# Three lanes of a four-layer graph network, emitted in finer turns

## The chip, the cores and the metric

The kernel runs on one core of a Trainium2 chip. The time is that of the device in microseconds (us), and the figure for a kernel is the median over several runs. A profile shows one execution. In it PE is the matrix engine (PEld: its weight loads, which overlap its matmuls), DVE the vector engine, ACT the scalar engine, POOL the GpSimd engine, and SP the engine that issues most DMAs. Each engine works through its own queue of instructions; semaphores order the engines among each other.

## The reference

There are 16 graphs of N = 1024 nodes with D = 128 features, each with a sparse weighted adjacency matrix `adj` (about 1.6% of the entries, and the diagonal, are not zero). Four layers follow each other. Each normalizes x over its features, takes the positive part as h, and adds to x what its network makes of h:

```python
# layer 0: mean over neighbours of h, joined to h, times W, relu
sum_neighbors = einsum('bid,bij->bjd', h, adj) / adj.sum(-1)
x += relu(concat([h, sum_neighbors]) @ W.T + b)
# layer 1: row-normalized adj times h, times W, leaky relu
x += leaky(einsum('bnm,bmf->bnf', adj / adj.sum(-1), h) @ W.T + b)
# layer 2, twice: a score for every pair of nodes, weighted messages, an update
hid = relu(a[:, :, None] + b[:, None, :] + be1)      # N x N x D
upd = adj * sigmoid(hid @ We2 + be2)
msg = upd @ x;  x = layernorm(x + relu([x, msg] @ Wu1 + bu1) @ Wu2 + bu2)
# layer 3: attention over neighbours
att = softmax(where(A > 0, leaky((Wh1 + Wh2.T) * A), -inf));  x += elu(att @ Wh)
```

## The kernel before

**Tiles.** The nodes of a graph are T = 8 tiles of P = 128. The pairs (t, u) of tiles are 36 buckets: 28 off the diagonal, 8 on it. In a bucket a row has few entries, so layer 2 is not computed for all pairs of nodes. `build` makes, for each bucket, four one-hot matrices in fp8: `on` and `om` say which node of tile t, and which of tile u, each entry (edge) has; `onT` and `omT` are their transposes. An off-diagonal bucket holds up to 320 such columns, a diagonal one 480.

**The work of layer 2** goes by nine groups of four buckets and twice over them, since layer 2 has two rounds. For each bucket, `gather` multiplies the node terms (`part`, split in two fp16 halves) by the one-hot matrices into a PSUM bank `pre` (of which there are two), four matmuls a bank; ACT takes the positive part to `hid`, and DVE the remainder to its second half. Off the diagonal this is done in both directions, d = 0 and 1. `dots` sums four `hid` tiles over the features into `sc`. `ends` applies tanh into `srow`. One group later `scores` transposes it (`pt`), and DVE multiplies `onT` and `omT` by the scores, tile by tile, into `val`: eight such multiplications an off-diagonal group, four a diagonal one. `scatter`, one quarter at a time, turns `val` back into a matrix of tiles in the bank `p`, DVE multiplies it by the loaded `adj` into `upd`, and `messages`, called later from the list `late`, adds up the messages in the banks `acc0` and `acc1`. `behind` is what calls these for the group before. `between` is the update of one half of the nodes between the two rounds: it loads the old features `xm`, evacuates the messages with `off`, runs `update` (two matmul stages `h` and `xn`, transposes `tx`, a normalization) and transposes the result (`tp`, L1146).

**Three lanes.** Three graphs are worked on at a time, each by a generator:

- `main` (lane m): layer 2 of graph b.
- `first` (lane a): layers 0 and 1 of graph b+1, and then `build` for it. For each of eight row tiles it loads `at` (rows) and `ct` (columns), transposes `at` on PE (`tn`), writes the transpose to DRAM, marks the buckets in `has`, and multiplies neighbours (`nb`), whose result DVE adds to `own`. Lane a has a single PSUM bank in the steady state, so `tn`, `nb`, and later `pr`, `pn`, `pq` and `pm` of `build` use it in turn.
- `last` (lane c): the second update of graph b-1, then layer 3, in which a strip `a` of adjT is loaded, DVE and ACT make `e` of it, and PE multiplies it (`hp`).

**What sets the order.** `weave` runs the three generators together. A generator's `yield us` says how much of its own time the turn just emitted is worth; divided by the lane's total (`MAIN_US`, `FIRST_US`, `LAST_US`) it gives the lane's progress, and the lane that is least far goes next. The sums of the turns are close to these constants, so all three lanes reach their end nearly together:

```python
least = min(out_of, key=lambda v: v[:2])
us = next(least[2], None)
...
least[0] += us / least[3]
```

This is not yet the order on the engines. The framework's planner gives each engine its queue, taking instructions as they become ready by its own costs, and among the ready ones those that were emitted first. It also hands out the buffers: two for `pre`, one for lane a, two rows of 512 KB for lane a's loads.

**Head and tail.** For graph 0 lane a runs alone up to the start of `build`; after graph 15's layer 2, lane c runs alone.

The lines that the prediction speaks of: L743 `tn`, L288 `nb`, L313 `own`, L260 transposes of the normalized input, L817 `pn` and `pm`, L850 `pq`, L854 `omT`, L986 `pre`, L1003 `hid` on DVE, L1018 `sc`, L1075 `val`, L1097 `p`, L1105 `upd`, L1114 `msg`, L342 `h`, L716 loads of `xm`, L1146 `tp`.

Of the kernel before, what the change touches and what calls it, by code (L numbers as in the profile page):

```python
# [42 lines left out]
MAIN_US = 243.0  # L43
FIRST_US = 118.0
LAST_US = 75.0
# [6 lines left out]
def tile_four_gnn_layers(  # L52
# [136 lines left out]
    class Layers:  # L189
# [74 lines left out]
        def pre_ln(self, xt, name, dst=None, dstT=None):  # L264

            h = self.scratch(f"h_{name}") if dst is None else dst
            self.normal(xt, h, AF.Relu, name)
            return self.transposed(h, name, dstT)
# [33 lines left out]
        def layer0_own(self, xt, name):  # L302
            hT = self.pre_ln(xt, f"0_{name}")
            z = self.scratch(f"z0_{name}")
            own = self.scratch(f"own_{name}")
            for sl, ps in self.both(hT, wT[:, 0:2], f"0_{name}"):
                nc.scalar.activation(z[:, sl], ps[:, :, 1], AF.Copy)
                nc.vector.tensor_add(own[:, sl], ps[:, :, 0], over_t(b0_bc, 2))
            return z, own
# [10 lines left out]
        def layer1(self, xt, strip, rdeg, name):  # L320
            hT = self.pre_ln(xt, f"1_{name}")
            yield 6
            z = self.scratch(f"z1_{name}")
            for sl, ps in self.by_node(hT, wT[:, 2], f"z1_{name}"):
                nc.scalar.activation(z[:, sl], ps, AF.Copy)
            o = self.scratch(f"o1_{name}")
# [57 lines left out]
        def layer3(self, xt, row, name):  # L384

            hT = self.pre_ln(xt, f"3_{name}")
            yield 6
            wh = self.scratch(f"wh_{name}")
            for sl, ps in self.by_node(hT, w3_sb, f"wh_{name}"):
                nc.scalar.activation(wh[:, sl], ps, AF.Copy)  # L390
            wh1, wh2 = self.score_terms(hT, 0, name)
# [70 lines left out]
    class Lane(Layers):  # L462
# [5 lines left out]
        def layer3(self, xt, strip, zero, name):  # L468
# [3 lines left out]
            hT = self.pre_ln(xt, f"3_{name}")  # L472
            yield 6
            wh = self.wide(f"wh_{name}")
            nc.vector.memset(wh[:, :, D : D + 1], 1.0)
            for sl, ps in self.by_node(hT, w3_sb, f"wh_{name}"):
                nc.scalar.activation(wh[:, sl, :D], ps, AF.Copy)
            wh2, wh1 = self.score_terms(hT, 1, name)
            yield 6
# [3 lines left out]
            for lo, hi in L3_ROWS:  # L483
# [4 lines left out]
                for k in range(0, T, 2):  # L488
# [13 lines left out]
                    nc.vector.scalar_tensor_tensor(e, at, 0.0, e, op0=OP.is_gt, op1=OP.mult)  # L502
                    for i in range(2):
# [5 lines left out]
                    yield 1.2 * n  # L509
# [18 lines left out]
    class Edges:  # L528
# [190 lines left out]
        def first(self, b):  # L719
# [4 lines left out]
            z, own = lane.layer0_own(xt, name)  # L724
            yield 8
# [6 lines left out]
            for t in range(T):  # L732
# [8 lines left out]
                for ks, ps in lane.halves(f"tn_{b}_{t}"):  # L741
                    for i, k in enumerate(ks):
                        nc.tensor.transpose(ps[:, i], at[:, k], ident)  # L743
                    nc.scalar.activation(turned[:, ks[0] : ks[-1] + 1], ps, AF.Copy)
                nc.sync.dma_start(self.columns(s.adjT, t), turned)
# [8 lines left out]
                yield 2  # L754
# [9 lines left out]
            s.xT = self.kept(lane.pre_ln(xt, f"2_{name}", dst=s.xf), "xT", f"xT0_{b}")  # L764
            s.x = self.kept(xt, "x", f"xk_{b}")
            yield 6
# [56 lines left out]
        def build(self, s, has, name):  # L823
# [4 lines left out]
            yield 0  # L828
            for g, grp in enumerate(GROUPS):
# [11 lines left out]
                nc.scalar.activation(rank, pr, AF.Copy)  # L841
                for i, (t, u) in enumerate(grp):
                    nm = f"{name}_{t}_{u}"
                    on = self.rows_hot(s, t, u, nm)
                    pn = self.turned(on, ck, f"pn_{nm}")
                    onT = self.hot_tile("onT", t, u, ck * P, nm)
                    nc.scalar.activation(onT, pn[:, : ck * P], AF.Copy, saturate=False)  # L847
                    pq = self.a.one(f"pq_{nm}").rearrange("p (k m) -> p k m", m=P)
# [9 lines left out]
                    )  # L858
                    pm = self.turned(omT, ck, f"pm_{nm}")
# [6 lines left out]
                    yield 1.3  # L866
# [14 lines left out]
        def round(self, s, l, name, before, after):  # L881
# [7 lines left out]
            def behind(i):  # L889
                if i == 0 and old:  # L890
                    old.scores()
                    parts.extend((old, part) for part in range(Q))
                elif parts:
                    g, part = parts.pop(0)
                    g.scatter(part)
                if len(self.late) > 1:
                    self.late.pop(0)()

# [4 lines left out]
            for k in range(len(GROUPS)):  # L903
# [9 lines left out]
                for i in range(Q):  # L913
                    g.gather(i)
# [3 lines left out]
                    behind(i)  # L918
                    g.dots()
                    yield 2.8  # L920
                    if (k, i) == (FIRST + 2, 1):
                        flush()
                        beside = after()
                    yield from islice(beside, 2)
                g.ends()
                old = g
            for i in range(Q + 2):
                behind(i)
# [483 lines left out]
```

## Time and profile before

| | |
|---|---|
| median of 3 runs | 5530.16 us (5516.44 to 5542.56) |
| the profiled execution, its own time | 5528.34 us |
| its span, first to last instruction | 5526.6 us |
| mean granted clock of PE | 0.987 |
| DMA, mean over the span | 100 GB/s |
| starts of `main` for graphs 5, 6 and 7 (its first load) | 1801.0, 2138.8, 2476.5 us |

The last row shows the period: 337 us a graph from graph 2 on, with three graphs in work at any moment. In what follows the head is 0 to 140 us, the tail 5400 us to the end, and the body what lies between. Rows of the view by stretches give the start and end of a stretch, its length, then for PE, PEld, DVE, ACT and POOL the busy time and the number of instructions, and at the end the granted clock, the share of DMA engines busy, and GB/s. Rows of the view of waits name who waited, for whom, the idle time in us, how often, and the longest. In the view in order of time the number in brackets is the idle time of the engine ahead of that row, and what ended it. An f32 matmul is two instructions in the trace.

### The profile page before, as it was taken

To read this page: it belongs to the slowest core of one execution; us is meant where nothing else is said; L and a number is where in the kernel's file an instruction comes from. 1 tells how busy PE (TensorE), PEld (TensorE's weight loads), DVE (VectorE), ACT (ScalarE), POOL (GpSimd) and SP (SyncE) were. 2 spreads that over 40 slices of the span, in tenths; PEclk is the share of its full clock that TensorE was granted. 3 is DMA by queue.
4 is the path that set the end of the run, shared out by engine and by line. 5 is a ranking of instruction groups with operands and counts; after the bars stand their busy time and mean duration, and the time that the engine had idled before them with its cause. 6 is when DMAs were issued, how large, how long until landed. Compare 5 with 4: busy or idle time off the path is not lost.

```text
span 5526.6 us, 113576 instructions
## 1 busy us (share of the span) xinstructions
PE 5037.3 (91%) x45109; PEld 3719.3 (67%) x45109; DVE 4304.6 (78%) x10759; ACT 3054.6 (55%) x6790; POOL 184.9 (3%) x137
## 2 busy tenths in 40 slices
PE   5999999999999999999999999999999999999996
PEld 4676766667676666666766666676766767666664
DVE  4777787878879787787877878778787887978886
ACT  4555564655647555465555646556465564655543
POOL 0000000000000000000000000000000000000000
PEclk8999999999999999999999999999999999999998
DMA  6242424243242433424334142432424324243111
GB/s 174 62 136 87 121 68 137 76 125 101 84 140 66 125 96 92 131 66 120 98 102 124 56 139 81 122 106 71 140 72 128 97 85 133 67 124 95 54 63 51
DMA packets 740139, 554.56 MB, mean 100 GB/s; under 512 B 32272, under 2 KB 686352, under 8 KB 739600
## 3 DMA queue, kind: packets, MB, share of 16 engines
q1 hardware_dynamic: 734496, 545.58, 33.6%
q8 instruction: 356, 5.83, 0.4%
q10 hardware_dynamic: 5104, 1.65, 0.1%
q14 instruction: 183, 1.50, 0.1%
HBM read 446.44 MB, written 100.66 MB: 99 GB/s over the span
## 4 chain that ended last, share of the span: by engine, by line
PE 47%; DVE 27%; DMA 9%; ACT 9%; issue 4%; POOL 3%; SPq 0%; ACTq 0%; DVEq 0%; POOLq 0%
PE pre L986 11%; DVE val L1075 10%; PE p L1097 6%; DMA at<-in_adj_dram 4%; DVE hid L1003 4%; PE nb L288 4%; PE msg L1114 4%; PE bb L296 3%; PE sc L1018 3%; DMA a<-adjT 2%; DVE omT L854 2%; PE hp L505 2%; POOL st L243 2%; PE h L342 2%; PE tn L743 2%
## 5 line engine op out<-in xcount | busy, mean ns | idle before, releaser
L1003 DVE SCALAR_TENSOR_TENSOR hid<-pre,hid 128x320 f16<-128x320 f32 (+1 forms) x2048 | 993.0, 504 | 294.9 <-ACT hid L1002 283.9
L1002 ACT ACTIVATE hid<-pre 128x320 f16<-128x320 f32 (+1 forms) x2048 | 900.7, 454 | 501.3 <-PE pre L986 473.4
L986 PEld LDWEIGHTS <-part 128*128 128x128 f16 x8192 | 753.4, 98 | 450.5 <-issue 236.2
L986 PE MATMUL pre<-on,part 128*128 128x320 fp8e4 (+1 forms) x4096 | 966.2, 309 | 71.6 <-DVE hid L1003 60.6
L986 PE MATMUL pre<-om,part 128*128 128x320 fp8e4 (+1 forms) x4096 | 994.3, 309 | 0.0
L1114 PE MATMUL msg<-upd,xf 128*128 128x128 f32 (+3 forms) x3008 | 613.6, 323 | 2.2 <-DVE upd L1105 2.2
L1075 DVE TENSOR_TENSOR val<-onT,u 128x384 f32<-128x384 fp8e4 (+1 forms) x1152 | 607.8, 580 | 4.0
L1097 PE MATMUL p<-val,omT 128*128 128x128 f16 x6528 | 534.2, 219 | 29.8 <-DVE val L1075 27.7
L1097 PEld LDWEIGHTS <-omT 128*128 128x128 fp8e4 x6528 | 436.7, 96 | 84.4 <-DVE val L1075 34.4
L1075 DVE TENSOR_TENSOR val<-omT,u 128x384 f32<-128x384 fp8e4 x896 | 439.2, 549 | 0.0
L861 ACT ACTIVATE om<-pm 128x320 fp8e4<-128x320 f32 (+1 forms) x576 | 268.9, 467 | 294.4 <-PE pm L817 285.8
L1114 PEld LDWEIGHTS msg<-upd,xf 128*128 128x128 f32 x3008 | 414.2, 191 | 25.6 <-DVE upd L1105 13.9
L1105 DVE SCALAR_TENSOR_TENSOR upd<-p,adj 128x512 f32<-128x512 f32 x512 | 348.5, 681 | 82.4 <-PE p L1097 82.2
L1097 PE MATMUL p<-val,onT 128*128 128x128 f16 x4480 | 374.1, 219 | 1.4 <-DVE upd L1105 1.4
L847 ACT ACTIVATE onT<-pn 128x384 fp8e4<-128x384 f32 (+1 forms) x576 | 297.6, 517 | 102.7 <-PE pn L817 82.8
L1039 ACT ACTIVATE srow<-sc,be_s,down 128x128 f32<-128x128 f32 (+2 forms) x512 | 259.7, 540 | 168.2 <-PE sc L1018 166.9
L505 PE MATMUL hp<-wh,e 128*128 128x129 f32 x2048 | 318.3, 285 | 22.3 <-DVE e L502 22.3
L1097 PEld LDWEIGHTS <-onT 128*128 128x128 fp8e4 x4480 | 304.6, 97 | 36.9 <-issue 8.8
L505 PEld LDWEIGHTS hp<-wh,e 128*128 128x128 f32 x2048 | 275.5, 195 | 51.9 <-DVE e L502 29.6
L804 ACT ACTIVATE far<-iota_off,mid 128x384 f16<-128x384 f16 x448 | 269.5, 625 | 39.9 <-DVE on L808 34.3
L288 PE MATMUL nb<-z,ct 128*128 128x128 f32 x2048 | 279.3, 282 | 12.4 <-DMA ct<-in_adj_dram 11.9
L1018 PE MATMUL sc<-hid,slide 128*32 128x320 f16 (+1 forms) x4096 | 268.3, 315 | 18.2 <-DVE hid L1003 15.7
(220 smaller groups left out, 8106.8 us busy)
## 6 DMA issues: line engine op xcount, KB each, us to landing
at<-in_adj_dram SPq DMA_DIRECT2D x128, 512.0 KB, 4.3
ct<-in_adj_dram SPq DMA_DIRECT2D x128, 512.0 KB, 4.6
adjT<-tn SPq DMA_DIRECT2D x128, 512.0 KB, 5.1
l<-adjT SPq DMA_DIRECT2D x128, 512.0 KB, 4.2
adj<-adjT SPq DMA_DIRECT2D x256, 256.0 KB, 3.4
a<-adjT SPq DMA_DIRECT2D x128, 384.0 KB, 3.5
adj<-adjT SPq DMA_DIRECT2D x448, 64.0 KB, 2.1
adj<-adjT SPq DMA_DIRECT2D x192, 128.0 KB, 2.6
```

The lines of the kernel that those rows point to most:

```text
L288: nc.tensor.matmul(ps, mat[:, k], z[:, k], start=(k == 0), stop=(k == T - 1))
L505: nc.tensor.matmul(sums[:, t], e[:, i, t * P : (t + 1) * P], wh[:, k + i, : D + 1], start=False, stop=True, skip_group_check=True,)
L804: nc.scalar.activation(far[:, : ck * P], self.iota[t == u][:, : ck * P], AF.Abs, bias=s.mid[:, i : i + 1])
L847: nc.scalar.activation(onT, pn[:, : ck * P], AF.Copy, saturate=False)
L986: nc.tensor.matmul(pre[:, :c], path.parts[node // Q][:, k, node % Q, v], hot[:, :c], start=(hot is on and k == 0), stop=(hot is om and k = ...
L1002: nc.scalar.activation(hid[:, 0, :c], pre[:, :c], AF.Relu)
L1003: nc.vector.scalar_tensor_tensor(hid[:, 1, :c], pre[:, :c], 0.0, hid[:, 0, :c], op0=OP.max, op1=OP.subtract)
L1018: ins = nc.tensor.matmul(self.sc[g * G : (g + 1) * G, : self.c], self.path.slide[:, self.l, G - 1 - r : 2 * G - 1 - r], self.hid[self.done ...
L1075: nc.vector.tensor_tensor(pair[:, i % 2, :ck], right[:, :ck], v.to_broadcast([P, ck, P]), op=OP.mult)
L1097: nc.tensor.matmul(self.ps[d][:, i], left[:, k], halves[:, k, :, h], start=(k, h) == terms[0], stop=(k, h) == terms[-1],)
L1105: nc.vector.scalar_tensor_tensor(upd, self.ps[d], S_SCALE, self.adj[:, d * Q : (d + 1) * Q], op0=OP.add, op1=OP.mult,)
L1114: nc.tensor.matmul(self.msg[h][:, (lo - h * Q) * P : (hi - h * Q) * P], self.xf[mb // Q][:, mb % Q], up, start=False, stop=True, skip_grou ...
```

## The change

The computation stays the same. Turns are cut smaller and given new worth, and some instructions change their place:

- `pre_ln` becomes a generator: the normalization is one turn, the transposes another. `layer0_own`, `layer1` and `layer3` hand its turns on.
- In `first`, `tn` yields after each half, and `nb` follows the second half in the same turn.
- In `build`, a bucket is five turns rather than one.
- In lane c's layer 3, a turn ends between the making of `e` and its matmuls, and between the two halves of these.
- In `round`, a gather of two directions, the scatter, the late messages and the dots are turns of 0.2 to 0.6, where before they were one turn of 2.8. `between` for half 0 is begun two gathers earlier (at group FIRST + 1, last bucket), but only up to a new `yield 0` behind its load.
- `last` issues the loads of both halves, and `off` for both, ahead of the first update; before, `main` did `off` at its end, and each half's load stood ahead of its own update.
- The three constants are set to the new sums.

```diff
-MAIN_US = 243.0
-FIRST_US = 118.0
-LAST_US = 75.0
+MAIN_US = 184.0
+FIRST_US = 115.0
+LAST_US = 70.0
...
-        def pre_ln(self, xt, name, dst=None, dstT=None):
+        def pre_ln(self, xt, name, dst=None):
             h = self.scratch(f"h_{name}") if dst is None else dst
             self.normal(xt, h, AF.Relu, name)
-            return self.transposed(h, name, dstT)
+            yield 2
+            self.hT = self.transposed(h, name)
+            yield 2
...
         def layer1(self, xt, strip, rdeg, name):
-            hT = self.pre_ln(xt, f"1_{name}")
-            yield 6
+            yield from self.pre_ln(xt, f"1_{name}")
             z = self.scratch(f"z1_{name}")
-            for sl, ps in self.by_node(hT, wT[:, 2], f"z1_{name}"):
+            for sl, ps in self.by_node(self.hT, wT[:, 2], f"z1_{name}"):
                 nc.scalar.activation(z[:, sl], ps, AF.Copy)
+                yield 1
...
                     nc.vector.scalar_tensor_tensor(e, at, 0.0, e, op0=OP.is_gt, op1=OP.mult)
+                    yield 0.4 * n
                     for i in range(2):
                         for t in range(n):
                             nc.tensor.matmul(
...
-                    yield 1.2 * n
+                        yield 0.4 * n
...
-            z, own = lane.layer0_own(xt, name)
-            yield 8
+            for _ in lane.layer0_own(xt, name):
+                if b:
+                    yield 1.3
+            z, own = lane.z, lane.o
+            yield 0
...
                     nc.scalar.activation(turned[:, ks[0] : ks[-1] + 1], ps, AF.Copy)
+                    yield 1
...
-                yield 2
                 lane.layer0_tile(t, ct, z, own, rdeg, name)
                 yield 2
...
                     on = self.rows_hot(s, t, u, nm)
+                    yield 0.1
                     pn = self.turned(on, ck, f"pn_{nm}")
                     onT = self.hot_tile("onT", t, u, ck * P, nm)
                     nc.scalar.activation(onT, pn[:, : ck * P], AF.Copy, saturate=False)
+                    yield 0.35
                     pq = self.a.one(f"pq_{nm}").rearrange("p (k m) -> p k m", m=P)
...
+                    yield 0.35
                     pm = self.turned(omT, ck, f"pm_{nm}")
...
-                    yield 1.3
+                    yield 0.35
...
                 if i == 0 and old:
                     old.scores()
                     parts.extend((old, part) for part in range(Q))
+                    yield 0.3
                 elif parts:
                     g, part = parts.pop(0)
                     g.scatter(part)
+                    yield 0.6
                 if len(self.late) > 1:
                     self.late.pop(0)()
+                    yield 0.5
...
                 for i in range(Q):
-                    g.gather(i)
+                    yield from g.gather(i)
                     if i == 0 and parts:
                         h, part = parts.pop(0)
                         h.scatter(part)
-                    behind(i)
+                        yield 0.6
+                    yield from behind(i)
                     g.dots()
-                    yield 2.8
-                    if (k, i) == (FIRST + 2, 1):
+                    yield 0.2
+                    if (k, i) == (FIRST + 1, Q - 1):
+                        beside = after()
+                        yield from islice(beside, 1)
+                    elif (k, i) == (FIRST + 2, 1):
                         flush()
-                        beside = after()
-                    yield from islice(beside, 2)
+                    if (k, i) < (FIRST + 1, Q - 1) or (k, i) >= (FIRST + 2, 1):
+                        yield from islice(beside, 2)
...
                     self.hid.append(hid)
+                    yield 0.6
...
             self.back(xT, oldT)
+            yield 0
             self.off(msg, msgT)
...
-            s.pairs = [self.c.scratch(f"xm_{b}_{h}") for h in range(NH)]
-            for h in range(NH):
-                self.off(self.msg[h], s.pairs[h][:, Q:])
+            s.msg = self.msg
...
             lane = self.c
+            pairs = [self.halves_of(lane.scratch(f"xm_{b}_{h}")) for h in range(NH)]
+            for h, (xT, msgT) in enumerate(pairs):
+                self.back(xT, s.xT[h])
+                self.off(s.msg[h], msgT)
+            yield 0
             new = lane.scratch(f"y_{b}")
             for h, dst in enumerate(self.halves_of(new)):
-                xT, msgT = self.halves_of(s.pairs[h])
-                self.back(xT, s.xT[h])
+                xT, msgT = pairs[h]
                 yield from lane.update(L - 1, s.xf[h], xT, msgT, dst, f"{b}_{L - 1}_{h}")
```

## The prediction

> **What bounds the kernel now.** I began with the busy shares of the page, cut them into head, body and tail, and then read the chain of waits of TensorE (PE) alone.
>
> ```profile
> PE 5037.3 (91%) x45109; PEld 3719.3 (67%) x45109; DVE 4304.6 (78%) x10759; ACT 3054.6 (55%) x6790; POOL 184.9 (3%) x137
> ...
> 0.00:140.00 140.00, 81.89 (x537) 67.28 (x537) 58.05 (x219) 68.72 (x136) 8.13 (x13) 0.84 0.59 172
> 140.00:5400.00 5260.00, 4877.19 (x44042) 3594.85 (x44041) 4162.30 (x10346) 2949.21 (x6584) 173.07 (x121) 1.00 0.34 100
> 5400.00:5526.60 126.60, 78.27 (x533) 57.17 (x531) 84.25 (x196) 36.66 (x71) 3.65 (x3) 0.80 0.17 49
> ...
> 2380.00:2476.50 96.50, 87.37 (x880) 63.47 (x880) 87.22 (x209) 63.46 (x152) 1.64 (x1) 1.00 0.21 63
> ```
>
> In the body PE is busy 4877 of 5260 us and idle 383: that idle time, some 27 us for each of 14 alike batches of 337 us, is what the change can take. VectorE (DVE) follows at 79%, and in the last row, the end of one batch, it stands level with PE: there DVE is a second bound. Head and tail hold 106 us of PE's idle time, but the built order of PE's instructions is the same there before and after, row for row; they get nothing.
>
> ```profile
> PE pm L817 <- DVE omT L854: 65.6, 70, 1.9
> PE tp L260 <- ACT h L252: 63.1, 31, 12.7
> PE pre L986 <- DVE hid L1003: 60.6, 101, 2.1
> PE p L1097 <- DVE val L1075: 27.7, 58, 1.2
> PE tn L743 <- DMA at<-in_adj_dram: 21.8, 26, 2.1
> PE h L342 <- DMA xm<-xT: 19.5, 14, 2.1
> PE tp L1146 <- DVE xf L369: 16.5, 16, 1.1
> PE tn L743 <- DVE own L313: 15.0, 14, 1.1
> ```
>
> Counts of 14 or 16 are one stop per batch at a fixed place; 70 or 101 are spread. The next rows are a spread one in time order, and then how fast PE goes when nothing stops it.
>
> ```profile
> 2433.60 0.55 DVE L1075 TENSOR_TENSOR val<-omT,u 128x384 f32<-128x384 fp8e4 x1
> 2434.07 0.55 DVE L854 TENSOR_TENSOR omT<-pq,odd_off 128x384 fp8e4<-128x384 f32 x1
> ...
> 2434.67 0.34 PE L817 MATMUL pm<-eye,omT 128*128 128x128 f16 x3 [1.62 <-DVE omT L854]
> ...
> 5381.23 0.51 PE L1097 MATMUL p<-val,onT 128*128 128x128 f16 x6
> 5381.57 1.07 PE L1114 MATMUL msg<-upd,xf 128*128 128x512 f32 x2
> ```
>
> The 1.62 us stop is not `omT`'s own 0.55 us: `omT` stood in DVE's queue behind a `val`. Six `p` matmuls start within 0.34 us, 57 ns each, though one alone lasts 218: a stop costs 0.16 us beyond its recorded idle time, hidden in "busy".
>
> [...] matmul counts times their undisturbed steps come to about 4400 us of the body's 5260. [...] Here one issue of an `xm` load took 0.40 us as a median, 1.43 at most.
>
> **The change part by part.** Nothing is added or removed: both programs have 39342 Matmult and 30720 Ldweights instructions on PE, 6661 activations, 1858 loads and stores on SP. Only order moves. The planner that orders instructions fills PE by readiness and takes a lane's turns as priorities, so the turns in the code are no measure; I compared the built orders. For each matmul that waits I summed the undisturbed PE steps standing between it and the matmul that feeds its producers, and took from this the producers' own mean durations from the groups[...]. This leaves out queueing on DVE and ACT: it compares orders and is not a time. Waits that come out late: 1655 before, 358 us in sum; 1404 after, 291 us. Part by part, against the rows above:
>
> 1. *Loads of `xm`.* In the turn between layers half 0's load may start 3.9 us of PE work ahead of its matmul, against this landing time:
>
> ```profile
> DMA to landing us min/median/max: 2.5/3.7/5.6
> ```
>
> After, it is 22 us ahead. 19.5 us go, and 14 restarts of 0.16, 2: **−21.5**. On SP's queue this load now passes the four `adj` loads of the last group and one `a` load of lane c; their users stand 18 us of PE work or more behind, so 0.4 us of issuing costs nothing (2 us at a later batch's first `a` if that cover were gone). The last layer's two loads go the other way, behind four `adj` loads: their lead falls from 13.5 to 6.2 us, still over the greatest landing time. Their two evacuations `off`, 0.6 us each on ACT, move from the end of one batch to the start of the next, where ACT is busy 24 of 41 us: 0.
> 2. *First `at` tile of a batch.* 15 loads had 3.6 us of lead against a median landing time of 4.3; after, lead under 4 us is left for 5 of 128 (was 19). Of the body's 19.5 us (the head holds the rest) I take **−15**; bounds 0 and −19.5.
> 3. *`tn` behind `own`.* The one PSUM bank of lane a passes from `nb` to the next `tn`; the least slack of these grows from 0.44 to 1.46 us. 14 stops of 1.07 us: **−12** (0 to −15).
> 4. *Transposes after the update (L1146).* Slack 2.1 to 2.65 us, half a us on 14 stops: **−7**.
> 5. *Building the one-hot tiles* (`pn`, `pq`, `pm`). One bank in a ring, three trips a tile, 36 tiles a batch. Late `pm`: 239 to 174, 52 to 32 us; `pq` 86 to 72; `pn` 58 to 71. The recorded stops of `pm` are the long ones behind a `val`, on which the half-us turns don't bear: of 65.6 us I take **−12** (+10 to −30).
> 6. *Gathers and scatters.* `pre` behind `hid`: quarter with least slack 0.42 before, 0.37 after: 0. `p` behind `val`: 74 waits within half a us become 38: **−8**. `val` bursts of eight in a row on DVE go from 138 to 151: not divided.
> 7. *`tn`, `nb`, `bb` and `msg` behind evacuations.* Late sums 33 to 9 us; seen mostly on weight loads that a running matmul covers, so half: **−12**.
> 8. *What comes instead.* 14 transposes of layer 2's input come out late by 1.06 us (none before), `tx` by 4 us in all, and 14 loads of layer 1's `l` have 4.7 us of lead (6.3 before) against a landing time of 4.2 median, 8.1 greatest: **+18** (0 to +40).
> 9. *Restarts.* 15% fewer late waits; of the body's 502 stops over 0.15 us some 75, at 0.16 us: **−12**.
>
> Pre-norm (63.1 us, 37 in the body): the slack of layer 1's transposes stays at 11 us: 0, bounds 0 and −30.
>
> Sum −81.5. The profiled execution took 5528.3 us (span 5526.6 and 1.7 around it) and becomes 5447; the median stands 1.8 us over that execution: **5449 us**, −1.5%. The bare late sum (−66), with parts 1 and 2, gives −100: the same size.
>
> **The rivals.**
> *The change does less than it says.* For: 5 and 6 show the same slack within 0.1 us in the order's middle, as the planner had mixed the lanes already. Parts 1 to 4 stay (−55), 8 takes 18: −37, 5493. If these too are eaten up by new fixed stops, one per batch of 1 us costing 14: no change, 5530.
> *DVE becomes the bound: slower.* Place: DVE's in-order queue where `val`, `hid` and lane c's `e` meet. I set each DVE instruction at the last matmul that it or one before it waits for, and summed DVE's durations over each 10 us of PE work. What lies over 10 us was 441 us in all and is 539 after, 98 more. PE has two `pre` banks in reserve. If all of it came out as PE stops: +98 −55, 5573; it decides from 55/98, 56%, on. Against: over 40 us the sums are equal, 57 and 57, and the slack of `hid` doesn't shrink.
> *More than I count.* The late sum in full (−66), 250 restarts (−40) and parts 1 to 4 (−55): −161, 5369.
>
> **How the numbers follow.** Sum above 0.50, its own range 5400 to 5485; only the fixed stops 0.18; no change 0.10; DVE 0.13; more 0.09. About 0.5% (5502 to 5558) is what can be told from no change; a third of the 0.18 falls inside it. Faster 0.50+0.12+0.09 = 0.71; same 0.06+0.09 = 0.15; slower 0.13 and 0.01 of the no-change case, 0.14. The range 5375 to 5540 leaves out DVE's case and half of "more": 0.18.
>
> **What would show it.** Right: no row of `h` behind DMA `xm`; `tn` behind DMA and `own` under 8 us together; PE's idle time in the body about 315 us, with the same matmul steps; DVE busy unchanged at 4304 us. Wrong: `pre` behind `hid` over 90 us (DVE's case); a new row with a count of 14 to 16 over 15 us (part 8, most likely `tp` behind `xf`); or `pm` unchanged at 65 and idle time at 345 (less than it says).

## The result and the profile after

The changed kernel takes 5477.55 us (median of 4 runs, 5471.68 to 5483.75), against 5525.44 us for the kernel before in the same comparison (4 runs, 5516.44 to 5542.56). The ratio is 0.991, with an interval of 0.9882 to 0.9938: 48 us, or 0.9%, faster. The direction was right and the time lies in the forecast range; the gain is 0.6 of the forecast one.

The profiled execution took 5483.75 us, 44.6 less in span than that of before. First the busy times on the page of the kernel after, then its view by stretches, with the body from 140 us to 127 us ahead of the end, as it was cut before.

```profile
PE 5008.5 (91%) x45109; PEld 3741.4 (68%) x45109; DVE 4302.6 (78%) x10759; ACT 3055.7 (56%) x6790; POOL 174.4 (3%) x137
```

```profile
0.00:140.00 140.00, 82.46 (x520) 68.74 (x520) 56.53 (x216) 67.48 (x133) 8.12 (x13) 0.82 0.59 172
140.00:5355.00 5215.00, 4846.73 (x44050) 3614.17 (x44051) 4160.64 (x10347) 2950.52 (x6585) 162.63 (x121) 0.99 0.34 101
5355.00:5482.00 127.00, 79.31 (x542) 58.45 (x539) 85.45 (x198) 37.74 (x73) 3.65 (x3) 0.81 0.17 49
```

In head and tail PE's busy time is within about 1 us of that before, and DVE is as busy as it was (4304.6 before). The body is 45 us shorter. What the reader should see is where: PE's recorded idle time there is 5215.0 less 4846.7, 368.3 us, only 14.5 below that of before. Most of the gain is inside "busy", and the granted clock of the body stands at 0.99, where it was 1.00.

To split the body I used three terms, which together make up its length less a constant. *Idle* is PE's recorded idle time. *Half clock* is the time in which the granted clock was 0.5; half of it is counted as lost, an estimate from the pace of `pre` shown below. *Rest* is PE's busy time less that loss and less 4324 us. This constant is my estimate of the sum of all matmul counts times their undisturbed steps in the traces, such as the 57 ns of a `p` (the prediction had about 4400); it sets the level of the rest, and not the differences between kernels. The rest is what no row of the profile records: the slow starts that the prediction put at 0.16 us a stop, an estimate from 218 less 57 ns, would be in it, and matmuls that run longer than their step.

| body, us | idle | half clock | rest |
|---|---|---|---|
| before | 383 | 44 | 531 |
| after | 368 | 113 | 467 |

So −14.5 of idle time, +34 for the clock (half of 68), −64 of rest: −45 in all. The sum has to come out, since the rest is defined as what is left; it is the split that tells something.

The rows of the view of waits of PE that matter, kernel after (us in all, how often, the longest):

```profile
PE pre L1001 <- DVE hid L1018: 62.3, 91, 3.9
PE tp L260 <- ACT xf L252: 55.9, 16, 5.1
PE tp L260 <- ACT h L252: 44.0, 19, 12.7
PE pm L822 <- DVE omT L862: 35.9, 66, 1.7
PE p L1113 <- DVE val L1091: 33.7, 30, 1.6
...
PE sc L1034 <- DVE hid L1018: 24.9, 23, 1.8
PE pn L822 <- ACT om L870: 19.5, 54, 0.5
...
PE h L344 <- DMA xm<-xT: 14.0, 14, 2.2
...
PE pr L840 <- ACT om L870: 10.0, 28, 0.5
PE nb L290 <- DMA l<-adjT: 9.3, 11, 2.6
PE tn L748 <- DVE own L315: 8.1, 14, 0.9
PE tn L748 <- DMA at<-in_adj_dram: 6.4, 7, 1.7
```

In the kernel before, the second row was

```profile
PE tp L260 <- ACT xf L252: 13.9, 15, 5.3
```

Of these 13.9 us 8.6 were in the body; of the 55.9 now, 50.8 are. It is the wait of layer 2's input transposes for their normalization in `pre_ln`, once a batch. `pm` lost half of its 65.6. The load of `xm`, which was to vanish, is still there with its 14 stops.

One of the new stops, in time order (start, duration, then the engine; in brackets the idle time of the engine ahead of the row, and what ended it):

```profile
2318.88 0.83 PE L507 MATMUL hp<-wh,e 128*128 128x129 f32 x6
2319.16 0.67 DVE L361 TENSOR_TENSOR xf<-tx,xf 128x512 f32<-128x512 f32 x1
2320.62 0.15 DVE L242 TENSOR_SCALAR st<-st 128x8 f32<-128x8 f32 x1
2320.91 1.64 POOL L243 TENSOR_TENSOR st<-st,half_neg 128x8 f32<-128x8 f32 x1 [33.14 <-DVE st L242]
2322.78 3.18 ACT L252 ACTIVATE xf<-x,st 128x128 f32<-128x128 f32 x8 [3.26 <-DVE st L250]
2323.33 0.33 PE L260 MATMUL tp<-ident,xf 128*128 128x128 f32 x1 [3.62 <-ACT xf L252]
2325.97 0.74 PE L1001 MATMUL pre<-om,part 128*128 128x320 fp8e4 x2
```

DVE reaches the statistics of layer 2's input late, POOL's power takes 1.64 us, ACT's first tile follows, and the transpose, which is what PE starts next, waits for it: 3.62 us. The last row is a pair of `pre` matmuls 2.6 us later. It lasts 0.74 us, and the next pair starts 0.53 us after it; a pair of the same shape, just ahead of the stop, lasted 0.44, and was followed after 0.27. The granted clock, the last column but two in the rows by stretches, goes with it. In the traces of before and after it is 1 or 0.5, and changes only on a grid of 3.413 us, so I cut the place on that grid:

```profile
2317.88:2321.29 3.41, 1.84 (x14) 1.26 (x11) 3.28 (x20) 0.98 (x2) 0.38 (x1) 1.00 0.29 117
2321.29:2324.70 3.41, 1.37 (x10) 0.62 (x10) 2.12 (x12) 1.92 (x5) 1.52 (x2) 1.00 0.01 2
2324.70:2328.11 3.41, 3.41 (x14) 2.14 (x14) 2.48 (x9) 2.83 (x7) 0.91 (x1) 0.50 0.18 43
2328.11:2331.53 3.42, 3.38 (x31) 2.72 (x30) 3.42 (x8) 3.05 (x9) 0.00 (x0) 1.00 0.85 295
```

The stop lies across the first two stretches. In the second PE was busy 1.37 of 3.41 us, and the third runs at half clock. The grid keeps no fixed distance to the stop: the half-clock pieces of the 14 stops begin from 1.5 us before the stop's end to 1.7 us after it. Nor need PE be idle for a whole stretch. The kernel before has 44 us of half clock in its body and no stop there above 2.6 us. One of 2.09 us, of `h` behind its load, was enough:

```profile
3673.15:3676.56 3.41, 1.32 (x4) 0.68 (x4) 2.67 (x3) 0.00 (x0) 0.00 (x0) 1.00 0.63 193
3676.56:3679.98 3.42, 3.42 (x7) 1.25 (x6) 0.88 (x2) 1.69 (x3) 0.00 (x0) 0.50 0.40 157
```

The bodies of all fourteen traces of this document, cut on the same grid, show how far this goes. Of the stretches in which PE was busy less than 40% of the time, all 100 were followed by one at half clock; at 40 to 50% it was 112 of 158, at 50 to 60% 77 of 331, and at 60% or more 95 of 20,709. What decides in between is not shown. In the changed kernel the 14 stops of 3.6 us brought one or two such pieces each, 75 of the 113 us; half of that, 37 us, is about all that the clock cost more than before. So the new stop costs its row, +42 us, and nearly as much again.

### The profile page after: what moved, and what is told of

It is laid out like the page before. It is cut to its first block, busy times and chain, and to the rows that moved or that the text cites. A ratio compares the mean times of both kernels' runs of the same rounds, so it can differ in the third digit from the quotient of the medians.

```text
span 5482.0 us, 113604 instructions
## 1 busy us (share of the span) xinstructions
PE 5008.5 (91%) x45109; PEld 3741.4 (68%) x45109; DVE 4302.6 (78%) x10759; ACT 3055.7 (56%) x6790; POOL 174.4 (3%) x137
## 4 chain that ended last, share of the span: by engine, by line
PE 49%; DVE 28%; ACT 9%; DMA 8%; issue 4%; POOL 3%; SPq 0%; POOLq 0%; ACTq 0%; DVEq 0%
PE pre L1001 13%; DVE val L1091 8%; PE p L1113 6%; DMA at<-in_adj_dram 5%; DVE hid L1018 4%; PE msg L1130 4%; PE sc L1034 3%; PE bb L298 3%; PE h L344 3%; PE nb L290 3%; ACT hid L1017 2%; PE hp L507 2%; DVE omT L862 2%; POOL st L243 2%; PE pq L858 2%
## 5 line engine op out<-in xcount | busy, mean ns | idle before, releaser
L1018 DVE SCALAR_TENSOR_TENSOR hid<-pre,hid 128x320 f16<-128x320 f32 (+1 forms) x2048 | 1009.2, 507 | 327.5 <-ACT hid L1017 315.9
L507 PE MATMUL hp<-wh,e 128*128 128x129 f32 x2048 | 336.0, 289 | 25.5 <-DVE e L503 25.5
L1113 PEld LDWEIGHTS <-onT 128*128 128x128 fp8e4 x4480 | 307.8, 97 | 51.7 <-issue 16.5
L1034 PE MATMUL sc<-hid,slide 128*32 128x320 f16 (+1 forms) x4096 | 275.2, 317 | 27.5 <-DVE hid L1018 24.9
L862 DVE TENSOR_TENSOR omT<-pq,odd_off 128x384 fp8e4<-128x384 f32 x448 | 248.7, 555 | 57.5 <-PE pq L858 54.7
L744 ACT ACTIVATE tn<-at 128x1024 f32<-128x1024 f32 x128 | 135.3, 1057 | 270.5 <-DMA at<-in_adj_dram 238.8
```

The costliest lines, as they stand in the source:

```text
L507: nc.tensor.matmul(sums[:, t], e[:, i, t * P : (t + 1) * P], wh[:, k + i, : D + 1], start=False, stop=True, skip_group_check=True,)
L862: nc.vector.tensor_tensor(omT.rearrange("p (k m) -> p k m", m=P), pq[:, :ck], self.odd[t == u][:, :, None].to_broadcast([P, ck, P]), op=OP ...
L1018: nc.vector.scalar_tensor_tensor(hid[:, 1, :c], pre[:, :c], 0.0, hid[:, 0, :c], op0=OP.max, op1=OP.subtract)
L1034: ins = nc.tensor.matmul(self.sc[g * G : (g + 1) * G, : self.c], self.path.slide[:, self.l, G - 1 - r : 2 * G - 1 - r], self.hid[self.done ...
L1113: nc.tensor.matmul(self.ps[d][:, i], left[:, k], halves[:, k, :, h], start=(k, h) == terms[0], stop=(k, h) == terms[-1],)
```

## The experiments

Two theories on why the kernel got faster. *By its parts*: the finer turns and the earlier loads take away the stops that the prediction lists, and part 8 gives some back. *By the draw*: every edit to turns, and every change of a pacing constant, gives another order, in which other stops recur once per batch, 14 times a run; which ones come is not steered by the edit, and the change is one draw of many. The two theories differ on a kernel whose pacing constant alone is moved by 1%.

### A pacing constant alone

The kernel before, with nothing changed but lane m's sum:

```diff
-MAIN_US = 243.0
+MAIN_US = 246.0
```

> The kernel before with MAIN_US 246 in place of 243: no turn divided, no load moved, only lane m paced 1.2% slower, so the planner's order is drawn anew. Theory A (finer turns and early loads are what saves time): no change, 5510 to 5545 us, PE's idle time in the body 370 to 395. Theory B (any new order moves the time, by which stops recur once per batch): the same count that gave 358 us late before and 291 after gives 295 here, so some 5480 us, with idle time 335 to 355.

Measured: 5479.07 us, 0.9903 of before (0.9883 to 0.9924). It is as fast as the changed kernel, without any of its edits, and as fast as the count of late waits had said (5480). Two rows of its view of waits of PE:

```profile
PE tp L260 <- ACT xf L252: 36.4, 16, 5.1
...
PE h L342 <- DMA xm<-xT: 17.1, 14, 2.3
```

It even has the changed kernel's new stop, in a milder form. Its idle time is 345, its half clock 113, its rest 485.

```diff
-MAIN_US = 243.0
+MAIN_US = 240.0
```

> The kernel before with MAIN_US 240 in place of 243. Theory A: no change, 5510 to 5545 us. Theory B: the late sum is 386 (before: 358), with the transposes between the rounds (tp behind xf of the update) 14 times late by 2 us: 5550 to 5570 us, and a row of 25 us or more for that wait (16.5 before).

Measured: 5488.68 us, 0.9925 (0.9901 to 0.9948). I had expected it slower, since its sum of late waits is the largest of all, 386 us: a miss. Its waits of PE show that other stops came:

```profile
PE sc L1018 <- DVE hid L1003: 40.6, 44, 1.8
...
PE tp L260 <- ACT hT L261: 23.7, 14, 1.7
```

`sc` behind `hid` was 15.7 us at 243, and `tp` behind `hT` 6.6; the wait of `tp` for `xf` is as good as gone (1.5 us in the body).

Then the changed kernel, with its constant moved by the same per cent:

```diff
-MAIN_US = 184.0
+MAIN_US = 182.0
```

> The changed kernel with MAIN_US 182 in place of 184 (lane m paced 1.1% faster). Theory B (the time is one draw of the order, moved by 40 us by any constant): not the time of the changed kernel within noise; with the slack of the layer-2 input's transposes back at +0.1 us the row tp behind xf falls from 50.8 to under 20 us, and the time lies between 5440 and 5475. Theory A (finer turns give a stable gain over coarse ones, whose draws at 240, 243 and 246 gave 5489, 5531 and 5479): 5470 to 5490.

Measured: 5510.66 us, 0.9965 of before (0.9951 to 0.9979). Neither theory's range holds this. The row of `tp` behind `xf` did fall as forecast, to 24.0 us (18.9 in the body), but `sc` behind `hid` rose from 24.9 to 58.4: with the new stop mostly gone the kernel was 33 us slower.

```diff
-MAIN_US = 184.0
+MAIN_US = 186.0
```

> The changed kernel with MAIN_US 186. Theory B: late sum 331 (291 in the changed kernel), the layer-2 input's transposes late by 2 us 14 times (1.06 in the changed kernel): a row of 55 to 80 us for tp behind xf and 5500 to 5530 us. Theory A: 5470 to 5490.

Measured: 5577.9 us, 1.0081 (1.0065 to 1.0098): slower than before. Not by the stop that I had expected to grow. Its waits of PE:

```profile
PE pre L1001 <- DVE hid L1018: 91.6, 114, 2.3
PE pm L822 <- DVE omT L862: 58.6, 96, 1.7
PE sc L1034 <- DVE hid L1018: 57.3, 22, 3.5
...
PE tp L260 <- ACT xf L252: 16.9, 16, 5.3
```

What follows: with coarse turns 240, 243 and 246 give 5489, 5531 and 5479 us; with fine ones (the turns of the change) 182, 184 and 186 give 5511, 5478 and 5578. The means are 5500 and 5522, the spreads 52 and 100. So the 48 us between 243 and 184 are no proof that the edits as a whole help: the kernel before sat on the worst of its three draws, and the changed one on the best of its own. At 186 the changed kernel looks like what the rival of DVE described: `pre` and `sc` behind `hid` stand at 149 us where before had 76, though DVE's busy time in the body (4164 us) is that of every other kernel.

### The loads

The earlier loads alone, in the kernel before:

```diff
-                    if (k, i) == (FIRST + 2, 1):
-                        flush()
+                    if (k, i) == (FIRST + 1, Q - 1):
                         beside = after()
-                    yield from islice(beside, 2)
+                        yield from islice(beside, 1)
+                    elif (k, i) == (FIRST + 2, 1):
+                        flush()
+                    if (k, i) < (FIRST + 1, Q - 1) or (k, i) >= (FIRST + 2, 1):
+                        yield from islice(beside, 2)
...
             self.back(xT, oldT)
+            yield 0
             self.off(msg, msgT)
```

with `last` as in the change, and `main` without its `off`.

> The kernel before with only the loads begun earlier (half 0's in round, both in last, off moved); turns and constants as before. The load theory of the prediction (part 1): h behind DMA xm falls from 19.5 to under 3 us, time 5500 to 5510. Rival: the stop of 1.4 us belongs to half 1, whose load isn't moved (its lead is 5.4 us of PE work before, 5.8 here): the row stays at 14 to 20 us, and the time goes by the new order alone; the count has tp behind xf of the layer-2 input late 14 times, so a row of 30 us or more there, and 5520 to 5560.

Measured: 5494.4 us, 0.9933 (0.9912 to 0.9953). Yet the row that this edit was to remove stands where it was, in its waits of PE:

```profile
PE h L342 <- DMA xm<-xT: 19.7, 15, 1.8
```

The gain, then, is not that of the row. The rival's row is right; its other two forecasts, a slower kernel and 30 us or more of `tp` behind `xf` (11.8 came), were not. The trace of the changed kernel shows the reason for the row. Issues on SP's queue, then the matmul that waits:

```profile
2303.33 0.43 SPq L984 DMA_DIRECT2D adj<-adjT  x1
2303.80 0.43 SPq L718 DMA_DIRECT2D xm<-xT  x1
2307.32 1.96 PE L344 MATMUL h<-xm,wu_sb 128*128 128x512 f32 x4 [0.84 <-DMA xm<-xT]
```

This batch's half 0 ran its `h` at 2276.31, with no stop. The load at 2303.80 is that of half 1, which neither kernel had moved ahead: it is begun in the second round, behind the `adj` loads of that round's group 1, and its matmul starts 3.5 us later. In the kernel before it is the same half, as its own trace shows, in each batch of the body:

```profile
2290.86 1.88 PE L342 MATMUL h<-xm,wu_sb 128*128 128x512 f32 x4
...
2326.59 1.96 PE L342 MATMUL h<-xm,wu_sb 128*128 128x512 f32 x4 [1.98 <-DMA xm<-xT]
```

So I moved half 1's load, in the changed kernel, to the start of the second round:

```diff
             old, new = None, self.Group(self, s, l, 0, msg, name)
+            yield from islice(beside, 1)
```

> The changed kernel with half 1's load between the rounds also begun ahead of use: one turn of its update (the load alone) ahead of the second round's first adj loads. Its lead grows from 5.9 to 12.4 us of PE work, and on SP's queue it stands before eight adj loads rather than behind them. If the stop of h behind DMA xm is this half's: 14.0 to under 2 us, and the time 12 to 16 us less, 5460 to 5467, if nothing else is drawn anew (late sum 287, was 291). Rival (the load isn't what h waits for): row and time unchanged, 5475 to 5485.

Measured: 5431.65 us, 0.9819 (0.9803 to 0.9835). In its waits of PE the row is gone; what is left of any `xm` load is

```profile
PE h L344 <- DMA xm<-xTk: 0.4, 1, 0.4
```

The same in the kernel before, with the new turn behind the load that it needs:

```diff
             old, new = None, self.Group(self, s, l, 0, msg, name)
+            yield from islice(beside, 1)
...
             self.back(xT, oldT)
+            yield 0
             self.off(msg, msgT)
```

> The kernel before, all turns as they were, with half 1's load alone begun ahead of the second round's adj loads. If that load is the one that h waited for: h behind DMA xm from 19.5 to under 3 us whatever the turns, and with it 15 to 40 us less, 5490 to 5515; if the time follows the order as a whole, it may lie anywhere from 5470 to 5540 with the row at 0 all the same. Rival (half 0's load as the prediction had it): the row stays at 14 to 20 us.

Measured: 5504.85 us, 0.9957 (0.9941 to 0.9974); the row goes from 19.5 to 0. What follows: in both kernels the stop is half 1's, and beginning that load earlier, ahead of the `adj` loads, removes it. Whether by its place in SP's queue or by its longer lead, these runs do not tell apart. In before the time falls by about the row (22 us); in after by 46 us against a row of 14, so that more came with the edit than this stop, as with any new order (idle time 335, rest 450).

### Lane m's turns

Lane m's finer turns alone, without loads, `build` and layers:

```diff
-MAIN_US = 243.0
+MAIN_US = 184.0
...
                 for i in range(Q):
-                    g.gather(i)
+                    yield from g.gather(i)
                     if i == 0 and parts:
                         h, part = parts.pop(0)
                         h.scatter(part)
-                    behind(i)
+                        yield 0.6
+                    yield from behind(i)
                     g.dots()
-                    yield 2.8
+                    yield 0.2
```

with the turns inside `behind` and `gather`, and `behind` at the end of a round, as in the change.

> The kernel before with only lane m's turns divided (gather, scatter, late messages, dots; MAIN_US 184). Theory A: most of the gain, 5480 to 5495, and p behind val and pre behind hid fall together from 88 to under 70 us. Theory B: the late sum is 350 (before 358), so no change within 25 us, 5505 to 5545, with tp behind xf of the update up from 16.5 to about 30 us.

Measured: 5518.45 us over 20 runs, 0.9975 (0.9969 to 0.9982). A quarter of a per cent, as theory B had it, from a split that is unlike that of before: idle time 373, half clock 126, rest 485. The finer turns in `build` and in the layers were not run alone.

### The stop at layer 2's input

If the stop of `tp` behind `xf` is what holds the changed kernel, more of lane m's work between normalization and transposes should end it. In the changed kernel:

```diff
-FIRST_US = 115.0
+FIRST_US = 121.0
...
             self.normal(xt, h, AF.Relu, name)
-            yield 2
+            yield 8 if dst is not None else 2
             self.hT = self.transposed(h, name)
```

Only layer 2's input has a `dst`, so the longer turn falls there alone. `FIRST_US` has to hold the longer sum, and so all other turns of lane a count for 5% less of its progress.

> The changed kernel with the turn between the layer-2 input's normalization and its transposes worth 8 in place of 2 (FIRST_US 121 to match), so that the transposes come later in lane a's turns. If the 50.8 us row is a matter of the place alone: it falls under 10 us, and the time by 40 us, to 5435 to 5450. If the normalization is slow because it meets that of the update on DVE and POOL, the wait moves with it: the row stays above 30 us, 5465 to 5485. The count gives slack +0.5 us (was -1.06), late sum 270, but tp behind xf of the update late by 13 us in all.

Measured: 5375.31 us, 0.9722 (0.9706 to 0.9738). Its row in the waits of PE is left with the single stop of the head:

```profile
PE tp L260 <- ACT xf L252: 5.1, 1, 5.1
```

The place that was shown above, in this kernel, in time order:

```profile
2266.74 1.64 POOL L243 TENSOR_TENSOR st<-st,half_neg 128x8 f32<-128x8 f32 x1 [25.12 <-DVE st L242]
...
2272.03 0.83 PE L507 MATMUL hp<-wh,e 128*128 128x129 f32 x6
2272.15 3.17 ACT L252 ACTIVATE xf<-x,st 128x128 f32<-128x128 f32 x8
2272.70 1.47 PE L260 MATMUL tp<-ident,xf 128*128 128x128 f32 x4
```

POOL's power, on the path before, now ends 3.7 us ahead of the `hp` matmuls; the transposes follow `hp` without a gap and run as four in a row. Against the changed kernel the body lost 71 us of idle time, 72 of half clock (36 us) and 3 of rest. The time fell by 102 us, more than the 40 expected, since the clock and other rows came on top. The row was 51 of the 71; the others that fell are `p` behind `val` (−18), `tp` behind `h` (−17) and `sc` behind `hid` (−14), while `at` and `tx` rose.

Does that hold on other draws? The same edit at 182 and 186:

```diff
-MAIN_US = 184.0
+MAIN_US = 182.0
```

> The changed kernel with the later transposes, and MAIN_US 182 in place of 184: the same step that made the changed kernel 33 us slower. If the later transposes hold against a new order: tp behind xf under 10 us, half-clock time under 60 us, 5375 to 5420. If 5375 was one lucky draw: 5430 to 5520, with another long stop in its place (the count has h2s and xn evacuations late by 31 us together).

Measured: 5361.97 us, 0.9706 (0.969 to 0.9723).

```diff
-MAIN_US = 184.0
+MAIN_US = 186.0
```

> The changed kernel with the later transposes, and MAIN_US 186: the step that made the changed kernel 100 us slower. Robust: tp behind xf under 10 us, half-clock time under 60 us (181 without the edit), 5375 to 5420 us. Lucky draw: 5430 to 5560.

Measured: 5402.84 us, 0.9775 (0.9758 to 0.9791). The three with this edit lie at 5362 to 5403, the three without at 5478 to 5578; no two overlap. This is the one edit shown to help on each of three draws. That its gain is mostly this stop and its clock is seen at 184 alone. At 182 it is worth 149 us and at 186 175 us, though the row itself was only 18.9 and 11.6 us of those kernels' bodies. At 186 the gain came with half clock of 72 rather than 181 us (under 60 was expected) and idle time of 330 rather than 426, so the edit does more than remove its own stop. That, I only see; I didn't take it apart. Nor was `FIRST_US` set to 121 without the longer turn, so the new pace of lane a may have a part in it.

Both edits that held, together:

> The changed kernel with both edits that shortened it: the layer-2 input's transposes later (worth 8) and half 1's load ahead of the second round's adj loads. If they remove two stops that have nothing to do with each other: h behind DMA xm 0 (14.7 with the first edit alone), tp behind xf under 5, half-clock time in the body about 40 us, and 5345 to 5365 us, the best so far. If each was a lucky order: anywhere from 5350 to 5450; the count gives late sum 281 and the transposes of the update 14 times late by 1.1 us.

Measured: 5355.38 us, 0.9693 of before (0.9677 to 0.9709). It is the fastest of all: 122 us below the changed kernel. Its stretch of the body, and its waits of PE:

```profile
140.00:5226.30 5086.30, 4804.92 (x44038) 3606.59 (x44036) 4171.12 (x10344) 2972.31 (x6584) 174.72 (x121) 0.99 0.35 103
```

```profile
PE tp L260 <- ACT hT L261: 30.6, 14, 2.2
...
PE pm L822 <- DVE omT L862: 26.5, 52, 1.7
...
PE tp L260 <- ACT xf L252: 5.3, 1, 5.3
```

Idle time in the body is 281 us, and a stop with a count of 14 has grown, `tp` behind `hT`, which was 6.5 us with the first edit alone. Half clock is 68 us, more than the 40 that I had expected. The time is in the range expected of two separate stops, but in that of a lucky order too.

### All in one table

Body times in us, in the order of the medians; "turns" says whether the turns are those of before (coarse) or of the change (fine). The median of before lay between 5525 and 5532 in the four comparisons.

| kernel | turns | median | idle | half clock | rest |
|---|---|---|---|---|---|
| `tp_and_half1` | fine | 5355 | 281 | 68 | 447 |
| `tp_182` | fine | 5362 | 312 | 10 | 450 |
| `after_late_tp` | fine | 5375 | 297 | 41 | 464 |
| `tp_186` | fine | 5403 | 330 | 72 | 446 |
| `after_half1` | fine | 5432 | 335 | 113 | 450 |
| after | fine | 5478 | 368 | 113 | 467 |
| `main_246` | coarse | 5479 | 345 | 113 | 485 |
| `main_240` | coarse | 5489 | 361 | 126 | 472 |
| `loads_only` | coarse | 5494 | 359 | 61 | 511 |
| `before_half1` | coarse | 5505 | 362 | 99 | 504 |
| `after_182` | fine | 5511 | 402 | 143 | 444 |
| `main_turns` | lane m fine | 5518 | 373 | 126 | 485 |
| before | coarse | 5525 | 383 | 44 | 531 |
| `after_186` | fine | 5578 | 426 | 181 | 472 |

The column that goes with the turns is the last: 472 to 531 with coarse turns (mean 500), 444 to 472 with all turns fine (mean 455). That is about 45 us on average; the two ranges touch. Idle time and half clock go with the order that was drawn. Why the rest falls is open. Fewer stops, each with the 0.16 us that the prediction estimated to be hidden in PE's busy time, would do it, but the recorded ones do not fit: the body of `after_182` has 573 stops over 0.15 us, that of before 502, and yet 87 us less of rest. No coarse kernel was run with layer 2's transposes put later; `main_240`, which hasn't that stop, still took 5489.

## Why the prediction was right and wrong

By size, it closes in three terms. Forecast: −68 of idle time in the body (383 to 315) and −14 for restarts. Measured: −14.5 of idle time, −64 of rest, and +34 for a clock that the sum did not hold. Idle fell 53 us short, rest gave 50 more, and most of the difference to the forecast is the clock's 34. The result lies in the range in part by luck: two large errors met, and of the three draws of the changed kernel one, at 5578, lies outside it.

Of the signs, DVE's busy time (4302.6 us) held. Idle time of 315, the vanished row of `xm`, and `tn` under 8 us did not. The sign of being wrong that part 8 named, a row of `tp` behind `xf` over 15 us with a count of 14 to 16, came.

1. *Loads of `xm`, −21.5*: wrong. The failing step is "half 0's load may start 3.9 us of PE work ahead of its matmul", taken as the cause of the row: the row was half 1's. It fell from 19.5 to 14.0 with the order, and `loads_only` left it at 19.7. The trace of before already had the stop at the second `h` of each pair. The signal "no row of `h` behind DMA `xm`" failed, and rightly showed it.
2. *First `at` tile, −15*: right in size, 19.5 to 4.0 in the body. But in whole runs `loads_only` has 6.2 us of this row with the old turns of lane a, and `after_late_tp` 21.0 with the new ones, so that the turns are not shown to be the cause.
3. *`tn` behind `own`, −12*: right in sign, 15.0 to 8.1, −7. Together with `at` 14.5 us were left where I had asked for 8. (In the changed code `nb` has a turn of its own behind that of `tn`'s second half; the section on the change puts both in one turn.)
4. *Transposes after the update, −7*: −15, 16.5 to 1.7.
5. *Building the one-hot tiles, −12*: about right as a sum, by terms I had not given: `pm` −30, `pq` −4, `pn` +9, `pr` +10, in all −15.
6. *Gathers and scatters*: `pre` 0 as said (60.6 and 60.8 in the body). `p` behind `val` was to fall by 8 and rose by 6; `sc` behind `hid`, which I did not price, rose by 10. The count of late waits leaves out the queue on DVE, and both of these wait for DVE.
7. *Evacuations, −12*: none of the rows concerned held more than 3.9 us before, so this could not come out of recorded idle time; if it came, it is in the rest, and nothing here tells it apart.
8. *What comes instead, +18*: right in kind and in place, `tp` behind `xf` 14 times a run, wrong in size. The term was mis-sized: it had 1.06 us a stop and none before; the stop grew by 3.0, from 0.6 to 3.6 (+42 in all). The count adds the producers' own durations and not the time that DVE takes to come to the statistics, which the rows above show to be late. With `l` (+9) and `hp` behind `e` (+4) it is +55, over the upper bound of 40, and some 37 us of clock come on top.
9. *Restarts, −12*: the stops over 0.15 us went from 502 to 479, 23 fewer and not 75, which at the estimated 0.16 us makes 4 us. The −64 of rest is something else, of which the draw is a part (`main_246` has −46 with coarse turns).

Pre-norm, 0: `tp` behind `h` fell by 19 us in the body, within the bound of −30. Part 1 to this, with all that came, sum to −6 of the −14.5 that were measured; what is left is in small rows. All these sizes are of one draw: at 186, in whole runs, `pm` stands at 58.6 us and `tn` behind `own` at 18.9, so that parts 3 and 5 are not shown to come from the turns either.

*The method.* The order-only sum of late waits did better as a ranking than as a time. For the nine kernels whose sum stands in the prediction or in an expectation: 386 us at 5489, 358 at 5531, 350 at 5518, 331 at 5578, 295 at 5479, 291 at 5478, 287 at 5432, 281 at 5355, 270 at 5375. The four over 300 are the slowest four; but the largest sum has the shortest time of these, and among the others 281 and 291 lie 123 us apart. `after_182`, at 5511 with a count of 286 that was not put down ahead of it, breaks the ranking. It found where a stop would come, and not how long it would last.

*The rivals.* "Less than it says" had 5493, near the result, by other means: its fixed stops gave −43 of the −55, but part 8 took 55 and not 18, and the rest made up for it. DVE's case, 5573, did not happen at 184 but is what 186 looks like (5578). What the prediction lacked was a rival by which the result is a matter of the draw; with a spread of 50 to 100 us for a per cent of pacing, it should have had the largest share after the sum.

## What to carry to other kernels

When a scheduler orders the work, move a pacing constant by 1% as a control before an edit is credited with a gain: here that alone gave 1.0%, where the change gave 0.9%. Then look for waits whose count equals the number of batches, ask which instance in the order they belong to, and give that one more distance: one longer turn at the right place, with its lane's constant, was worth more than all the finer turns. Stops are to be priced with the clock that they cost afterwards: here one of 2.09 us was enough, where it left PE busy for less than 40% of a stretch of 3.4 us.

## What was not expected of the hardware

- A single stop in the middle of a busy stretch brought 3.4 us at a clock of 0.5, or 6.8, though PE worked again at once: 3.62 us of stop did so in all 14 batches of the changed kernel, and one of 2.09 us in the kernel before. In these traces the clock followed PE's busy share in the 3.413 us before: under 40%, half clock in 100 cases of 100. Over the body this was 10 to 181 us of half clock, from kernel to kernel, with the same instructions.
- The power of a 128x8 tile on GpSimd took 1.64 us, the median of 64 in the changed kernel. It was the longest single step between the last statistics and the first normalized tile, and in the place shown it lay in the chain that PE waited behind.
- In the changed kernel a load that stands right behind another group's loads on SP's queue was issued 0.47 us after the last of them and waited for 14 times a run; begun at the start of the round, it is not waited for.
